# Gram's blocks written as products with ones, and running sums that begin with two tiles

## The chip, the cores and the metric

The kernel runs on one core of a Trainium2 chip. The metric is the device time of one execution in microseconds (us). Three runs of the kernel before gave 2723.8, 2724.28 and 2724.82 us; the median is 2724.28.

## What is computed

Eight images of 768 channels and 32 x 32 pixels go through two residual layers in float32. Cut to what matters:

```
h   = groupnorm(x)                        # 32 groups
k,v = h W_k, h W_v                        # 12 heads of 64; q is not needed
s   = var(v) var(k)^T / 8                 # one number per token and head: an outer product
x  += softmax(s) v  W_proj + b
f   = groupnorm(x)
c_o = sum_channels fn(p + o) fn(p)        # fn: f with unit norm, 28 offsets o in a 7 x 7 window
x  += [f, c] W_conv + b
```

The scores are an outer product of two vectors, so a tile of exponentials is one activation of a broadcast row with a per-partition scale. The softmax's denominators are sums of exponentials over keys. The correlations c are read from the diagonals of small Gram products of f with shifted windows of itself.

## The kernel before

**Staging.** The images are processed one after the other, with the stages of neighbours interleaved. In stage b the attention of image b, the second half of its keys and values, and the second layer (Gram products, then the convolution) of image b - 1 share the engines; "stage" always means this b, 0 to 8. TensorE (PE) runs the large products in a Strassen form with seven products in place of eight; sums of blocks for it are made by GpSimd (POOL) in `make_sums` (L579, instructions at L584 to L590) or by VectorE (DVE). ScalarE (ACT) makes the exponentials (L721). DVE takes results out of PSUM, does statistics and adds up denominators; its calls pass through a timing wrapper, so all of them carry line L152.

**Order.** The program is laid out by a planner in Python: `Clock` keeps a planned time for PE, ACT and DVE, units of work are emitted when their planned inputs are ready, and evacuations are emitted at planned due times. What the planner emits is a fixed order on each engine's queue; each queue runs in order, and semaphores make it wait for its operands. So a changed planned duration or a changed buffer release can reorder instructions on every queue.

**Attention.** A pair is two heads. `products(t)` (L740) multiplies the exponential tiles of key block t (two tiles of 128x1024) with the values, 8 matmuls in the trace, and eight blocks make a pair. `run` (L951) emits four blocks at a time, called a run of four here, and puts units of other stages between the runs. The pool of exponential tiles has six buffers (L175), three blocks' worth, so the exponentials of block t + 3 need the tiles of block t; `free_at` (L958) tells the planner when that will be. The denominators are had in two ways. For some pairs ACT makes the exponentials a second time, transposed, with a summed output (L731). For the summed pairs (L47: pairs 0, 3, 4, 5 of the first image, 3, 4, 5 of the others, 25 in all), DVE adds the eight tiles of each head into an accumulator `acc`, a copy for the first (L757) and seven additions (L759), and PE adds up its partitions at the end (`den`, L779 and L829). The accumulators take the buffers `bk` of the second exponentials (two, L174).

**Gram.** `turn(t)` (L1053) copies a block of 128 tokens of f, all six channel groups, into a tile in which the left and right halves of the image rows lie apart: two POOL copies of 128x384 (L1065), one for each half; the last image uses ACT. There is one such buffer (L176). `gram(t)` (L1067) multiplies the turned block with windows of f (L1080, 24 matmuls) and then emits the turn of block t + 1, which so waits for PE to be done with block t. Eight grams of an image lie between attention runs and units of keys and values. After grams 3 and 7, `diagonals` gathers the diagonals through DRAM and `scale` (L1119) turns the squared norms into reciprocal roots: a POOL `pow` on 128x4 (`rn`, L1125), then DVE makes the columns `dn`, and PE transposes them (`ct`, L1136).

**POOL's libraries.** The maximum over partitions in `spread` (`most`, L661) is a partition all-reduce of POOL. In the built kernel an instruction without a tile stands in front of each such all-reduce and in front of the first `tensor_tensor` after it: a change of POOL's instruction library. A POOL `tensor_copy` after the all-reduce has no such instruction in front. In stages 2 to 7 the first `tensor_tensor` after the all-reduce for the first half of the heads (`most_0`) is `rn` of the first four grams, behind the copies of turns 1 to 5:

```
POOL queue, before:  most_0 | turn_1 .. turn_5 (copies) | library change | rn_0 | turn_6
```

Of the kernel before, what the change touches and what calls it, by code (L numbers as in the profile page):

```python
# [8 lines left out]
ALU = mybir.AluOpType  # L9
# [7 lines left out]
J = C // P  # L17
# [11 lines left out]
HW = W // 2  # L29
# [42 lines left out]
def windows(ap, *dims):  # L72

    return bass.AP(tensor=ap.tensor, offset=ap.offset, ap=[list(d) for d in dims])
# [83 lines left out]
def two_layers(ctx, tc, x, wkv, wproj, bproj, wconv, wcorr, bconv, out):  # L158
    nc = tc.nc
# [29 lines left out]
    vector = Vector(nc.vector, clock)  # L189
# [23 lines left out]
    def act_copy(us, to, at):  # L213
        nc.scalar.copy(to, at)  # L214
        clock.act = max(clock.act, clock.now) + us
# [15 lines left out]
    class WeightSums:  # L231


        def __init__(self, which, *queues):
            self.which = which
            flat = image_tile(fpool, "f", f"ws{which}").rearrange("p j n -> p (j n)")
            self.at = [flat[:, n * JH * KW : (n + 1) * JH * KW] for n in range(5)]
            for n in range(4):
                r, c = divmod(n, 2)
                queue = queues[n % len(queues)]  # L240
                if which in (0, 1):
                    queue.dma_start(out=self.at[n].rearrange("p (k m) -> p k m", k=JH), in_=kv_block(which, r, c))
                else:
                    to = self.at[n].rearrange("p (k m) -> p k m", k=JH)
                    queue.dma_start(out=to, in_=t_block(which, r, c).rearrange("p k i m -> p k (i m)"))
# [145 lines left out]
    ones = const.tile([P, HD], F32, name="ones")  # L391
# [14 lines left out]
    rows = [dconst.tile([NROW, ROW], F32, name=f"rows{i}") for i in range(2)]  # L406
# [6 lines left out]
    def mask_rows():  # L413
        nc.gpsimd.memset(mask, 1.0)
        nc.gpsimd.memset(across, 1.0)
        at = 0
        for _, right, count in RUNS:
            run = across[:, at : at + count] if at else across[:, 0 : count - 1]
            right, count = (right, count) if at else (1, count - 1)
            for base, sign in ((right, 1), (W - 1 - right, -1)):  # L420
                nc.gpsimd.affine_select(
                    out=run, in_=run, compare_op=ALU.is_ge, fill=0.0, base=base,
                    pattern=[[sign, count]], channel_multiplier=sign,
                )
            at += count
        for q in range(P // HW):
            side = q // (P // W)
            nc.sync.dma_start(out=mask[q * HW : (q + 1) * HW, 1:], in_=across[side * HW : (side + 1) * HW, :])
# [262 lines left out]
    class Pair:  # L691
        def __init__(self, b, hp, kv, ot, before):
            half = hp // 3
            self.before, self.finished = before, False
            self.b, self.hp, self.half, self.vt, self.ot, self.kv = b, hp, half, kv.vt[hp], ot, kv
            self.summed = hp in SUMMED[b > 0]
            self.rows_at = {}
            self.over, self.rd_at, self.bk_free, self.out_at = False, None, False, None
            self.exs, self.bc, self.bk = {}, [], []
            self.passes = {"e": 0, "s": 0}  # L700
# [39 lines left out]
        def products(self, t):  # L740
            if t == 0:
                self.av = avp.tile([P, 2, HF], F32, tag="av", name=f"av{self.b}_{self.hp}")
            exs = self.exs.pop(t)
            for hf in range(2):
                for e in range(2):
                    nc.tensor.matmul(  # L746
                        self.av[e * HD : (e + 1) * HD, hf, :], lhsT=self.vt[:, t, e, :],
                        rhs=exs[e][:, hf * HF : (hf + 1) * HF], start=t == 0, stop=t == MT - 1,
                    )
            if t == MT - 1:  # L750
                later.after(STEP_US + 0.2, self.evacuate)
            if self.summed:
                if t == 0:
                    self.acc = [bkpool.tile([P, N], F32, tag="bk", name=f"acc{self.b}_{self.hp}_{e}") for e in range(2)]
                for acc, ex in zip(self.acc, exs):
                    if t == 0:
                        vector.tensor_copy(acc, ex)  # L757
                    else:
                        vector.tensor_tensor(acc, acc, ex, ALU.add)  # L759
                if t == MT - 1:  # L760
                    later.after_dve(0.5, self.sum_up if self.hp < HP - 1 else self.sum_up_last)
            if t == MT - 1:
                self.over = True
                self.try_finish()
# [108 lines left out]
    class Attention:  # L873
# [77 lines left out]
        def run(self):  # L951
            hp, t0 = divmod(self.done, MT)
            for t in range(t0, t0 + STEPS):
                while t not in self.pairs[hp].exs:
                    clock.pass_time(0.25)
                pair = self.pairs[hp]
                pair.products(t)
                self.free_at.append(max(clock.now + STEP_US, clock.dve - EXP if pair.summed else 0.0))  # L958
                self.done += 1
                clock.pass_time(STEP_US)  # L960

# [87 lines left out]
    class Corr:  # L1049
# [3 lines left out]
        def turn(self, t):  # L1053

            last = self.b == NB - 1
            pl, tag = (expool, "ex") if last else (turnpool, "turn")
            flat = pl.tile([P, N if last else J * P], F32, tag=tag, name=f"turn{self.b}_{t}")[:, : J * P]
            self.turned[t] = flat.rearrange("p (j s m) -> p j s m", j=J, s=2)
            to = flat.rearrange("p (j s y x) -> p j s y x", j=J, s=2, x=HW)
            rows = self.f[:, :, t * P : (t + 1) * P].rearrange("p j (y s x) -> p j y s x", y=4, s=2)  # L1060
            for side in range(2):
                if last:
                    act_copy(0.5, to[:, :, side], rows[:, :, :, side, :])
                else:
                    nc.gpsimd.tensor_copy(to[:, :, side], rows[:, :, :, side, :])  # L1065

        def gram(self, t):  # L1067

# [353 lines left out]
    for b in range(NB + 1):  # L1422
# [6 lines left out]
        if b:  # L1429
# [3 lines left out]
            f, acc = layer1[b - 1] if b > 1 else first_f * 2  # L1433
# [75 lines left out]
```

## Time and profile before

| | |
|---|---|
| median of 3 runs | 2724.28 us |
| profiled execution | 2723.3 us |
| its span on the core | 2721.6 us |
| PE busy | 2649.8 us (97%) |
| DVE busy | 1632.4 us (60%) |
| ACT busy | 1365.4 us (50%) |
| POOL busy | 355.3 us (13%) |
| granted PE clock, mean | 0.992 of full speed |

The span is from the first to the last instruction of the profiled execution; what lies around it is 1.7 us in that execution. The profile's groups name the operation by line, engine and tiles (buffer numbers left out), and tell how long the engine was idle before it and what ended that idle time. "Issue" is idle time that no semaphore of the profile explains. Matmuls are pipelined and their ends are modelled, so PE counts as busy over small gaps between matmuls.

### The profile page before, as it was taken

Reading aid. Unit: us, or ns where it says so; the run is one execution under the profiler, and the core shown is the slowest. Engines: PE = TensorE matmul, PEld = TensorE weight load, DVE = VectorE, ACT = ScalarE, POOL = GpSimd, SP = SyncE. Lnnn points to the kernel's source line nnn. Section 1 sums busy time; section 2 is a strip of 40 time slices with the busy share of each in tenths; the row PEclk is TensorE's granted clock in tenths of the full one; section 3 lists DMA queues with packets and bytes.
Section 4 is the critical chain, followed back from the end, with each engine's and each line's share of the span. In section 5 each row is a group of like instructions: output and inputs, shape, how many; then the busy total and the mean of one; then the engine's idle time right before and its main releaser. Section 6 shows DMA issues by size and latency. Waiting matters only on the chain.

```text
span 2721.6 us, 30651 instructions
## 1 busy us (share of the span) xinstructions
PE 2649.8 (97%) x9831; PEld 1230.9 (45%) x9831; DVE 1632.4 (60%) x4160; ACT 1365.4 (50%) x1841; POOL 355.3 (13%) x442
## 2 busy tenths in 40 slices
PE   7999999999999999999999999999999999999999
PEld 4443454345543454434544345443454434544344
DVE  5859734775347853478524875258742587525864
ACT  1497078700697006970079701796017960189600
POOL 4220120003200032000320012200122001220000
PEclk9999999999999999999999999999999999999999
DMA  7764456354553645626556365462654626545243
GB/s 275 297 233 134 142 191 179 105 201 154 158 180 112 205 152 157 194 90 210 158 153 191 92 208 167 141 205 79 223 167 139 189 82 230 172 116 158 86 127 101
DMA packets 323355, 446.04 MB, mean 164 GB/s; under 512 B 59458, under 2 KB 245170, under 8 KB 323194
## 3 DMA queue, kind: packets, MB, share of 16 engines
q1 hardware_dynamic: 321962, 441.32, 50.9%
q10 hardware_dynamic: 1232, 2.75, 0.3%
q8 instruction: 79, 1.29, 0.2%
q14 instruction: 82, 0.67, 0.1%
HBM read 377.49 MB, written 64.40 MB: 162 GB/s over the span
## 4 chain that ended last, share of the span: by engine, by line
PE 89%; DMA 5%; issue 3%; DVE 2%; ACT 1%; POOL 1%; SPq 0%; DVEq 0%; POOLq 0%; ACTq 0%
PE x L359 35%; PE av L746 22%; PE y L359 17%; PE z L359 9%; PE gr L1080 3%; DMA x<-x1d 1%; DMA di<-ir 1%; PE den L779 1%; DMA rd<-di 1%; PE x L988 1%; PE den L829 1%; PE y L988 1%; DMA vdr<-rsv 1%; PE z L988 1%; ACT ex L721 0%
## 5 line engine op out<-in xcount | busy, mean ns | idle before, releaser
L721 ACT ACTIVATE ex<-bc,nk 128x1024 f32<-128x1024 f32 x768 | 826.8, 1137 | 449.1 <-DMA bc<-vdr 227.0
L746 PE MATMUL av<-ex,v 128*64 128x512 f32 x3072 | 705.3, 604 | 4.8 <-ACT ex L721 4.6
L731 ACT ACTIVATE junk<-bk,vm 128x1024 bf16<-128x1024 f32 x368 | 420.4, 1142 | 42.1 <-DMA bk<-kdr 22.8
L746 PEld LDWEIGHTS av<-ex,v 128*64 128x64 f32 x3072 | 230.5, 138 | 442.7 <-issue 380.1
L152 DVE TENSOR_TENSOR acc<-acc,ex 128x1024 f32<-128x1024 f32 x350 | 402.0, 1215 | 0.0
L214 ACT COPY kp<-x 128x384 f32<-128x384 f32 x28 | 13.4, 478 | 559.2 <-PE x L359 559.2
L359 PE MATMUL y<-kv,s 128*128 128x384 f32 x744 | 260.7, 491 | 0.0
L359 PE MATMUL x<-kv,xn 128*128 128x384 f32 x756 | 257.1, 490 | 2.8 <-DVE xn L152 1.6
L359 PE MATMUL x<-kv,s 128*128 128x384 f32 x744 | 254.3, 489 | 0.0
L359 PEld LDWEIGHTS x<-kv,xn 128*128 128x128 f32 x756 | 144.1, 191 | 106.0 <-issue 7.1
L359 PEld LDWEIGHTS x<-kv,s 128*128 128x128 f32 x744 | 138.7, 190 | 101.9 <-issue 9.1
L359 PEld LDWEIGHTS y<-kv,s 128*128 128x128 f32 x744 | 137.8, 190 | 94.8 <-issue 7.3
L480 POOL TENSOR_TENSOR rstda<-vea,neghalf 128x1 f32<-128x1 f32 x8 | 4.8, 595 | 1009.9 <-DVE vea L152 1009.9
L359 PE MATMUL x<-v,wt 128*128 128x512 f32 x288 | 130.2, 596 | 0.0
L359 PE MATMUL z<-kv,xn 128*128 128x384 f32 x372 | 126.9, 488 | 0.0
L152 DVE TENSOR_TENSOR v<-y,v 128x128 f32<-128x128 f32 x180 | 40.9, 282 | 137.5 <-PE y L359 137.5
L359 PE MATMUL x<-f,wt 128*128 128x512 f32 x252 | 116.2, 601 | 1.9 <-DVE x L152 1.8
L584 POOL TENSOR_TENSOR s<-xn 128x384 f32<-128x384 f32 x64 | 68.0, 1070 | 290.2 <-PE x L359 202.2
L152 DVE BATCH_NORM_STATS2 vbn<-v 128x6 f32<-128x64 f32 x720 | 101.8, 211 | 0.0
L152 DVE COPY win<-gr 128x133 f32<-128x133 f32 x64 | 18.4, 288 | 128.2 <-PE gr L1080 118.6
L1065 POOL COPY turn<-f 128x384 f32<-128x384 f32 x112 | 54.5, 514 | 305.4 <-PE gr L1080 292.2
L152 DVE SCALAR_TENSOR_TENSOR x<-x,bconv_sb,x 128x512 f32<-128x512 f32 x63 | 45.8, 746 | 78.1 <-DMA x<-x1d 55.9
(191 smaller groups left out, 3040.3 us busy)
## 6 DMA issues: line engine op xcount, KB each, us to landing
kv<-kvs SPq DMA_DIRECT2D x124, 576.0 KB
kv<-in_wkv_dram SPq DMA_DIRECT2D x95, 576.0 KB
bc<-vdr SPq DMA_DIRECT2D x96, 512.0 KB
f<-in_x_dram SPq DMA_DIRECT2D x48, 512.0 KB
bk<-kdr SPq DMA_DIRECT2D x46, 512.0 KB
x1d<-f SPq DMA_DIRECT2D x42, 512.0 KB
x<-x1d SPq DMA_DIRECT2D x42, 512.0 KB
out_dram<-x SPq DMA_DIRECT2D x82, 256.0 KB
```

The costliest lines, as they stand in the source:

```text
L152: return getattr(self.engine, name)(*args, **kw)
L214: nc.scalar.copy(to, at)
L359: nc.tensor.matmul(t, lhsT=lhsT, rhs=rhs, start=p in FIRST and k == 0, stop=stop and k == len(pairs) - 1, skip_group_check=True,)
L584: nc.gpsimd.tensor_tensor(self.sums[g][:, 0], a[g][2], a[g][3], ALU.add)
L721: nc.scalar.activation(ex, self.bc[e], AF.Exp, scale=self.kv.nk[self.half][:, h, t : t + 1])
L731: nc.scalar.activation(junk, self.bk[e], AF.Exp, scale=self.kv.m2[self.half][:, h, t : t + 1], accum_out=self.sums[:, e, t : t + 1],)
L746: nc.tensor.matmul(self.av[e * HD : (e + 1) * HD, hf, :], lhsT=self.vt[:, t, e, :], rhs=exs[e][:, hf * HF : (hf + 1) * HF], start=t == 0, ...
L779: nc.tensor.matmul(den[at * 32 : (at + 1) * 32, :], lhsT=ones[:, 0:32], rhs=self.acc[e][:, hf * HF : (hf + 1) * HF], start=True, stop=True,)
L829: nc.tensor.matmul(den[e * HD : (e + 1) * HD, :], lhsT=ones, rhs=self.acc[e][:, at], start=True, stop=True)
L988: nc.tensor.matmul(t, lhsT=wcorr_sb[at, i, :], rhs=cs[at, tokens, :], start=False, stop=True, skip_group_check=True)
L1065: nc.gpsimd.tensor_copy(to[:, :, side], rows[:, :, :, side, :])
L1080: nc.tensor.matmul(ps[side * HD : (side + 1) * HD, :n].rearrange("p (y x) -> p y x", x=WIDE), lhsT=block[:, j, side, :], rhs=image[:, 4 * ...
```

## The change

In `turn`, the POOL copy becomes a POOL product of the same block with a tile of ones, read with a stride of zero over the six channel groups. In a summed pair, the copy of the first tile into the accumulator is gone: the addition at block 1 reads the tiles of blocks 0 and 1 and writes the accumulator. So the tiles of block 0 are now read by DVE at block 1, and the planner is told that they come free when those of block 1 do.

```
 class Pair:
-            self.before, self.finished = before, False
+            self.before, self.finished, self.first = before, False, []
 # products(t)
             if self.summed:
+                before = list(self.first)
                 if t == 0:
                     self.acc = [bkpool.tile(...) for e in range(2)]
                 for acc, ex in zip(self.acc, exs):
-                    if t == 0:
-                        vector.tensor_copy(acc, ex)
-                    else:
-                        vector.tensor_tensor(acc, acc, ex, ALU.add)
+                    if t:
+                        vector.tensor_tensor(acc, before.pop(0) if t == 1 else acc, ex, ALU.add)
+                self.first = exs
 # run()
                 self.free_at.append(max(clock.now + STEP_US, clock.dve - EXP if pair.summed else 0.0))
+                if pair.summed and t == 1:
+                    self.free_at[-2] = self.free_at[-1]
 # turn(t)
                 else:
-                    nc.gpsimd.tensor_copy(to[:, :, side], rows[:, :, :, side, :])
+                    half = rows[:, :, :, side, :]
+                    nc.gpsimd.tensor_tensor(to[:, :, side], half, windows(ones, ones.ap[0], (0, J), (HW, 4), (1, HW)), ALU.mult)
```

In the built kernel after the change, the library change of stages 2 to 7 stands directly behind `most_0` and in front of turn 1, and none is left in front of `rn_0`:

```
POOL queue, after:   most_0 | library change | turn_1 .. turn_5 (products) | rn_0 | turn_6
```

PE's order is the same in every stage up to the last runs of its attention. From pair 3 on (in stage 0 from pair 0 on) units of the convolution or of keys and values move by one to a few places: in stages 2 to 6 the eight blocks of pair 5, which stood in one piece of 64 matmuls, are now two runs of 32 with a unit between, and in stages 0 and 7 the same happens to pair 4.

## The prediction

> **What bounds the kernel now.** I read the page first. PE is busy 97% of a span of 2721.6 us and the chain that ended last is 89% PE, so time can come only from PE's gaps or from PE running slowly.
>
> ```profile
> PE 2649.8 (97%) x9831; PEld 1230.9 (45%) x9831; DVE 1632.4 (60%) x4160; ACT 1365.4 (50%) x1841; POOL 355.3 (13%) x442
> ```
>
> Second, the view of waits: for PE alone, and then over all engines for the last line.
>
> ```profile
> PE ct L1136 <- DVE dn L152: 33.4, 6, 6.2
> PE pma L465 <- DVE mva L152: 14.1, 1, 14.1
> PE av L746 <- ACT ex L721: 4.6, 4, 2.2
> PE den L779 <- DVE acc L152: 3.8, 2, 2.5
> PE gr L1080 <- POOL turn L1065: 2.9, 1, 2.9
> ...
> POOL rn L1125 <- issue: 45.5, 6, 8.2
> ```
>
> Columns: total us, times, longest. Nearly half of PE's 72 us of idle time is one transpose, `ct`, six times; 14.1 is the start. Behind `dn` stands POOL's `rn`, six times late for no semaphore ("issue"), 7.6 us each. Third, the timeline of stage 2, POOL and then PE (start, duration):
>
> ```profile
> 683.90 0.43 POOL L661 PARTITION_ALL_REDUCE most<-top  x1 [7.43 <-DVE top L152]
> 688.71 0.95 POOL L1065 COPY turn<-f 128x384 f32<-128x384 f32 x2 [4.37 <-PE gr L1080]
> ...
> 721.59 0.96 POOL L1065 COPY turn<-f 128x384 f32<-128x384 f32 x2 [8.49 <-PE gr L1080]
> 730.46 1.05 POOL L1125 TENSOR_TENSOR rn<-m,neghalf 128x4 f32<-128x4 f32 x1 [7.92 <-issue]
> ```
> ```profile
> 694.67 1.58 PE L1080 MATMUL gr<-f,turn 128*64 128x133 f32 x24
> ...
> 721.27 5.32 PE L746 MATMUL av<-ex,v 128*64 128x512 f32 x24
> 732.49 0.41 PE L1136 MATMUL ct<-ident,dn 128*80 128x128 f32 x1 [5.90 <-DVE dn L152]
> 732.83 3.19 PE L746 MATMUL av<-ex,v 128*64 128x512 f32 x8
> 735.86 1.53 PE L1080 MATMUL gr<-f,turn 128*64 128x133 f32 x24
> ```
>
> The turn's copies end at 722.55 and `rn` starts 7.92 later. That is where the built kernel has its library change. Also, the eight matmuls after `ct` take 3.03 us to the next row's start, where a quarter of a run of 32 (7.02) is 1.76. Fourth, the busy times by stretch (us; busy PE, PEld, DVE, ACT, POOL; granted clock; DMA) say why: the clock is 0.57 there, 0.50 to 0.57 in all six places.
>
> ```profile
> 721.20:726.20 5.00, 5.00 (x30) 1.64 (x24) 0.84 (x4) 3.02 (x4) 0.96 (x2) 1.00 0.44 162
> 732.40:735.90 3.50, 3.41 (x11) 1.09 (x13) 0.28 (x1) 0.00 (x0) 0.00 (x0) 0.57 0.09 26
> ```
>
> **What the Trainium skill says.** GPSIMD Engine Reference, 2.1 Instruction dispatch: the first call to a freshly loaded kernel pays about 6 us of load that shows as no instruction. The trace agrees in kind; here it is 7.2 to 8.2 us. The same page, 3.1 Elementwise: about 2.6 cycles for each element of a two-input operation, 1.03 for a simple one-input one. The trace: 1007 ns (two inputs, L590) and 514 ns (the copy), both 128x384. TensorE: Matmul & The Clock Gate, Part 1: after an idle window of about 3.4 us PE falls to half rate until it has been busy as long; the 0.57 above agrees. VectorE: DVE Perf Modes, the perf-mode tier table: an fp32 copy in SBUF runs at 2x, a tensor_tensor at 1x; 689 against 1220 ns (median) here.
>
> **Part 1, the library change moves.** Removed: one change of 7.2 to 8.2 us in front of `rn`, in six stages. In stage 2 the new `rn` starts when turn 5 is done: 721.59 + 2 x 1.01 = 723.6. It ends 1.05 later at 724.65. From the end of `rn` to `ct` takes 0.98 now (731.51 to 732.49), so `ct` could start at 725.65, and PE gets there at 732.49 - 5.90 = 726.59. Nothing is left of the wait, with 0.9 us to spare. In all six stages PE reaches `ct` 5.0 us after turn 5 starts. The gain is read from the first of the 24 matmuls to the gram after the eight: 14.59, 14.05, 15.32, 14.55, 14.02 and 14.28 us in the six stages, 86.8 in all; undisturbed it is a run of 7.02 and a transpose of 0.13 or so, 43 for six. Gain **43.6**: 33.4 of wait, the rest the slow clock after it. I take 43.
>
> Added: the change behind `most_0`. The all-reduce ends at 684.33; the change carries no wait of its own, so it starts there and ends at 691.5 to 692.5. Turn 1 waits behind it, 2.0 us for two products, until 693.5 to 694.5; gram 1 starts at 694.67. Hidden by the units of keys and values that PE has there, with 0.2 to 1.2 us to spare. Only turn 1 and gram 1 wait behind it on POOL, and all six stages have the same distance (10.8 us from all-reduce to gram 1). I put 0.1 us each, **+0.6**; if the change took 1 us more here, +5.
>
> **Part 2, products for copies.** 112 POOL instructions by 1007 - 514 = 493 ns is 55 us more on an engine at 13%. Covered where PE has other work before the next gram, which is 3 us or more after a turn nearly everywhere (694.67 and the next one 7.5 later, say). Not covered: the first gram of stage 1 (the wait of 2.9 on the turn), +1.1 for two slower halves, and its gram 2 (+0.1). The product with a zero-stride operand is not in the trace of before: bounds 0.8 us (2.6 cycles for 384 elements without dispatch) and 1.5 us (the slowest copy, 1500 ns); at 1.5 the six gram 1 would each wait 0.0 to 0.8 and `ct` 0.1. I take 1.01. **+1.2**.
>
> **Part 3, no copies into the accumulator.** 50 copies by 0.69 is 34.5 us less on DVE, which bounds no stage. The addition at block 1 costs what it did; only an operand differs. So directly nothing. Two indirect effects:
>
> *The tile of block 0 is held longer.* In a summed pair with run start T, steps on PE last 1.76. DVE first clears two evacuations and a reciprocal (to T + 1.6), adds head 0 to T + 2.8 and head 1 to T + 3.95. ACT's exponentials of block 3 (1.14 each) then end at T + 4.05 and T + 5.2; now the first starts at T + 2. PE needs them at T + 5.27 and about T + 5.5. It fits by 0.3 us. If that cover is gone, each 1 us costs 25 pairs by 1. The later blocks: block 6 is ready at T + 11.65 and needed at T + 13.4; `den` of pair 3 needs the last addition at T + 18.4 and PE comes at T + 20.6. I walked pairs 4 and 5 likewise in the order of the built kernel and found no wait.
>
> *The order of PE's queue.* The planner counts a copy at 1.2 us, so 2.4 us of planned DVE time go per pair, and runs and units move by a few places. PE's work is the same; what changes is whether a pair of 64 matmuls stands in one piece, where ACT (2.14 us per block by its rows) cannot follow PE (1.76):
>
> ```profile
> 1201.68 7.09 PE L746 MATMUL av<-ex,v 128*64 128x512 f32 x32
> ...
> 1212.46 14.94 PE L746 MATMUL av<-ex,v 128*64 128x512 f32 x64
> ```
>
> To the next row's start it is 14.87, against 2 x 7.02: 0.83 lost. Four of stages 2 to 6 lose 0.83, the fifth 15.77 - 14.04 = 1.73; all five are split now. **-5.0**. Pair 4 of stage 7 loses 15.76 - 14.04 = 1.7 with its wait for the accumulator; split, **-1.7**. In stage 0 pair 4 stood in one piece too (17.7 with 2.5 waiting for `acc`); in two runs with 3.9 us of units between, DVE's 16.1 of additions and some 2.5 of evacuations end 0.8 us after PE: **-3**. The new order may have waits that I haven't found; I take back 2.
>
> **The sum.** -43 + 0.6 + 1.2 - 9.7 + 2 = -49 on the span of 2721.6. The execution around it was 2723.3, the median 2724.28, 1.0 more. So 2724.3 - 49 = 2675.3; I say **2676**.
>
> **Rivals.** (a) *The change turns into a wait at gram 1.* For it: less than 1 us to spare, and DMA is half busy around 684 to 692. Against it: the change ran at a like DMA load (0.41 to 0.46) where it stood. With 1 to 2 us in six stages, 5 to 12: 2681 to 2688. (b) *Only the wait goes, and the reordered attention gives nothing* (new small waits at held tiles equal what the splits gain): -43 + 2 to -33 + 2, 2683 to 2693. (c) *Slower: held tiles.* DVE is in order, so if a reciprocal of 1.7 us or a DMA-bound one stands before the additions of block 1, block 3 comes late in each summed pair. It decides from (43 + 8) / 25 = 2 us per pair, that is if DVE starts those additions 2.3 us later than I walked. Against it: DVE idles 5.12 us in front of pair 4's copies in stage 2. At 3 us: 25 x 2.7 = 68, less 49, is 2743. (d) *The library change isn't what made `rn` late*, and it stays late behind slower turns: -9.7 + 2 + 1.2, and 1 us more at each of six `ct`, 2724. Against it: of 16 `rn` only the six with a change in front have this gap.
>
> **Chances.** Forecast 0.66; (a) 0.14; (b) 0.16; (c) 0.02; (d) 0.02. The range from 2666 (no waits at all and stages 0 and 7 gaining more) to 2692 holds the forecast and nearly all of (a) and (b), some 0.86. Within 0.2% (5.4 us), about what a measurement here can tell from no change, only (d) falls: faster 0.96, same 0.02, slower 0.02.
>
> **What would show it.** Right: `ct` gone from PE's waits, no "issue" in front of `rn`, granted clock near 1 after `ct`, some 7 us of idle in front of turn 1 behind `most_0`, gram 1 not later than 10.8 us after the all-reduce. Wrong: PE waits for `turn` six times (a), for `ex` or `acc` in runs of pairs 3 to 5 (b, c), or `rn` still late (d).

## The result and the profile after

The changed kernel took 2679.46 us (median of 4 runs, 2675.76 to 2680.35), beside 2724.04 for the kernel before (2719.56 to 2724.82). The ratio is 0.9837, with a 95% interval of 0.982 to 0.9854. The forecast was 2676, and the interval times 2724.04 runs from 2675 to 2684. A second set of runs gave 2679.13 and a ratio of 0.9844 (0.983 to 0.9859). The profiled execution took 2675.76 us around a span of 2674.0, so it is the shortest of the first four runs and flatters the change a little.

The page of the kernel after, busy time by engine:

```profile
PE 2634.8 (99%) x9831; PEld 1221.7 (46%) x9831; DVE 1604.2 (60%) x4110; ACT 1364.0 (51%) x1841; POOL 410.8 (15%) x442
```

POOL is busy 55.5 us longer with its 112 products, and DVE 28.2 us shorter without its 50 copies. PE is busy 15.0 us *shorter* with the same 9831 instructions: part of the gain is matmuls that run faster, not waits that are gone. The view of waits of the kernel after, for PE (us in total, times, longest):

```profile
PE pma L465 <- DVE mva L152: 13.8, 1, 13.8
PE av L746 <- ACT ex L721: 5.6, 4, 2.8
PE gr L1083 <- POOL turn L1068: 3.9, 2, 3.4
PE x L359 <- DVE x L152: 3.4, 7, 0.5
...
PE den L779 <- DVE acc L152: 1.2, 1, 1.2
```

`ct`, the first line of this view before, is gone. The start (`pma`) is what it was. The wait for `turn` has grown by 1.0 us and is met twice, not six times. PE's waits for `x` from DVE have grown, from three (1.8 us) before to seven (3.4 us). The timeline of stage 2, POOL and then PE (start, duration):

```profile
683.12 0.43 POOL L661 PARTITION_ALL_REDUCE most<-top  x1 [7.43 <-DVE top L152]
691.27 1.97 POOL L1068 TENSOR_TENSOR turn<-f,ones 128x384 f32<-128x384 f32 x2 [7.72 <-issue]
...
720.81 1.97 POOL L1068 TENSOR_TENSOR turn<-f,ones 128x384 f32<-128x384 f32 x2 [7.47 <-PE gr L1083]
722.74 1.06 POOL L1128 TENSOR_TENSOR rn<-m,neghalf 128x4 f32<-128x4 f32 x1
```
```profile
693.89 1.58 PE L1083 MATMUL gr<-f,turn 128*64 128x133 f32 x24
...
720.49 5.32 PE L746 MATMUL av<-ex,v 128*64 128x512 f32 x24
725.74 0.31 PE L1139 MATMUL ct<-ident,dn 128*80 128x128 f32 x1
725.97 1.94 PE L746 MATMUL av<-ex,v 128*64 128x512 f32 x8
727.74 1.53 PE L1083 MATMUL gr<-f,turn 128*64 128x133 f32 x24
```

The 7.72 us of idle time without a semaphore now stand in front of turn 1, and `rn` follows turn 5 at once. Turn 1 ends at 693.24 and gram 1 starts at 693.89, so 0.65 us were to spare; gram 1 is 10.77 us behind the start of the all-reduce, as before (694.67 - 683.90). The eight matmuls after `ct` take 1.77 us to the next row's start, and the busy times by stretch (PE, PEld, DVE, ACT, POOL; granted clock; DMA) show why:

```profile
725.40:728.90 3.50, 3.50 (x33) 1.90 (x33) 0.29 (x1) 3.50 (x7) 0.00 (x0) 1.00 0.80 226
```

The granted clock is 1.00 here, where it was 0.57. "Half clock" below means a stretch in which the trace's record of the granted clock reads 0.50.

### The profile page after: what moved, and what is told of

It is laid out like the page before. It is cut to its first block, busy times and chain, and to the rows that moved or that the text cites. A ratio compares the mean times of both kernels' runs of the same rounds, so it can differ in the third digit from the quotient of the medians.

```text
span 2674.0 us, 30536 instructions
## 1 busy us (share of the span) xinstructions
PE 2634.8 (99%) x9831; PEld 1221.7 (46%) x9831; DVE 1604.2 (60%) x4110; ACT 1364.0 (51%) x1841; POOL 410.8 (15%) x442
## 4 chain that ended last, share of the span: by engine, by line
PE 93%; DMA 4%; DVE 2%; issue 0%; ACT 0%; SPq 0%; POOL 0%; DVEq 0%; POOLq 0%; ACTq 0%
PE x L359 36%; PE av L746 24%; PE y L359 17%; PE z L359 9%; PE gr L1083 3%; DMA x<-x1d 1%; PE den L779 1%; PE x L990 1%; PE y L990 1%; PE z L990 1%; DMA vdr<-rsv 0%; DMA x1d<-f 0%; DVE x L152 0%; DVE v L152 0%; PE den L829 0%
## 5 line engine op out<-in xcount | busy, mean ns | idle before, releaser
L746 PE MATMUL av<-ex,v 128*64 128x512 f32 x3072 | 691.7, 597 | 5.6 <-ACT ex L721 5.6
L746 PEld LDWEIGHTS av<-ex,v 128*64 128x64 f32 x3072 | 223.4, 137 | 434.8 <-issue 372.4
L152 DVE TENSOR_TENSOR acc<-acc,ex 128x1024 f32<-128x1024 f32 x300 | 344.7, 1211 | 0.0
L1068 POOL TENSOR_TENSOR turn<-f,ones 128x384 f32<-128x384 f32 x112 | 111.6, 1016 | 265.9 <-PE gr L1083 206.5
L359 PEld LDWEIGHTS z<-kv,xn 128*128 128x128 f32 x372 | 69.9, 190 | 49.2 <-issue 2.3
```

The lines of the kernel that those rows point to most:

```text
L152: return getattr(self.engine, name)(*args, **kw)
L359: nc.tensor.matmul(t, lhsT=lhsT, rhs=rhs, start=p in FIRST and k == 0, stop=stop and k == len(pairs) - 1, skip_group_check=True,)
L746: nc.tensor.matmul(self.av[e * HD : (e + 1) * HD, hf, :], lhsT=self.vt[:, t, e, :], rhs=exs[e][:, hf * HF : (hf + 1) * HF], start=t == 0, ...
L1068: nc.gpsimd.tensor_tensor(to[:, :, side], half, windows(ones, ones.ap[0], (0, J), (HW, 4), (1, HW)), ALU.mult)
```

## The experiments

The kernels ran in four groups, each on one chip with the kernel before beside it, whose medians were 2723.49, 2721.39, 2721.87 and 2723.16 us. Kernels of different groups are compared by their distance from it. Each kernel starts from the one before or the one after, with the edit shown.

**The products alone.** Only the part of the change in `turn` is made, and the copies into the accumulators stay. PE's order is that of before.

> Only Gram's blocks as products with ones (parts 1 and 2); the copies into the accumulators stay, and PE's order is that of before. The prediction's theory (the moved library change takes the wait at ct away, the reordered attention gives the rest): 43 us less, 1.8 more for the slower turns, so 2683 us; ct gone from PE's waits, pair 5 of stages 2 to 6 still one piece that loses 0.8 to 1.7 us. Rival (the products as such give everything, the sums nothing): 2679, like the full change. Rival (the library change isn't the cause): 2724 or more.

Measured: 2683.12 us (2680.13 to 2686.23), ratio 0.9849 (0.9835 to 0.9862), 40.4 less than before. The prediction has -41.2 for parts 1 and 2.

**The sums alone.** All of the change is made except its part in `turn`: the running sums begin with two tiles, and the turns stay copies. PE's order is that of after.

> Only the running sums that begin with two tiles (part 3); the turns stay copies, so the library change stays in front of rn, and PE's order is that of the full change. The prediction's theory: the six waits at ct stay (33 us in all, half clock after them) and only the split pairs gain, -9.7 + 2, so about 2716 us. Rival (the attention's order gives nothing): 2724. Rival (held tiles cost time): over 2726.

Measured: 2725.15 us (2716.74 to 2726.53), ratio 1.0 (0.9991 to 1.0008): nothing, where 7.7 us less was expected. The wait at `ct` stays (view of waits, sums alone):

```profile
PE ct L1138 <- DVE dn L152: 32.3, 6, 6.0
```

To find where the gain went, I summed the times from one matmul's start to the next's, by product, over stages 2 to 6 (from one `most_0` to the next), and divided by five. Per stage, before and sums alone:

```
                 before   sums alone   difference
attention av      92.18      91.39       -0.79
Gram gr           11.16      11.71       +0.55
conv. y<-f         8.30       8.91       +0.61
conv. x<-t4f       8.02       8.32       +0.30
it                 0.33       0.43       +0.10
whole stage      335.61     336.41       +0.80
```

The split pairs do gain: 0.8 us in each stage here, and 0.7 in the kernels below that have no wait at `ct` (84.85 to 84.16 us of `av` with the tiny product). The Gram's 0.55 is the half clock after `ct`, which lasts 6.83 us in all six stages here and in three of six before. In the row `y<-f` two waits of PE for a tile `x` from DVE are hidden. The first stands in front of `x<-f`, 124 to 133 us behind `most_0`. It comes and goes between executions of one kernel, in either order: 2.6 us over stages 2 to 7 before, 2.1 here, 5.9 and 1.2 in two executions of the products alone. The second is new, and the reordering makes it. The timeline of stage 2, DVE and then PE, in the kernel before:

```profile
895.29 1.22 DVE L152 TENSOR_TENSOR v<-v,rd 128x1024 f32<-128x1024 f32 x1
899.61 1.76 DVE L152 RECIPROCAL acc<-den 128x256 f32<-128x256 f32 x1 [3.10 <-PE den L829]
901.28 0.63 DVE L152 TENSOR_TENSOR x<-z,x 128x512 f32<-128x512 f32 x1
901.83 0.68 DVE L152 TENSOR_TENSOR x<-x,x 128x512 f32<-128x512 f32 x1
```
```profile
903.00 2.74 PE L359 MATMUL x<-t4f,wt 128*128 128x512 f32 x6
```

The same place with the sums alone:

```profile
902.80 1.76 DVE L152 RECIPROCAL acc<-den 128x256 f32<-128x256 f32 x1 [4.54 <-PE den L829]
904.49 1.23 DVE L152 TENSOR_TENSOR v<-v,rd 128x1024 f32<-128x1024 f32 x1
905.63 0.68 DVE L152 TENSOR_TENSOR x<-z,x 128x512 f32<-128x512 f32 x1
906.24 0.68 DVE L152 TENSOR_TENSOR x<-x,x 128x512 f32<-128x512 f32 x1
```
```profile
906.97 2.84 PE L359 MATMUL x<-t4f,wt 128*128 128x512 f32 x6 [0.61 <-DVE x L152]
```

Before, DVE does the product `v<-v,rd` in front of the reciprocal, in time in which it would idle for `den` anyway; the result tile `x` is out at 902.51, half a microsecond before PE is there. In the new order the product stands behind the reciprocal, the idle time grows from 3.10 to 4.54, and `x` is out 4.12 us after the reciprocal's start where it was 2.90. PE, which comes to the tile at about the same distance, waits. This place loses 0.67 to 0.84 us in each of stages 2 to 7 in all five profiled executions with the new order, and nothing in the nine with the old one. The 0.30 of `x<-t4f` and the 0.10 of `it` come with the new order every time, too; they were not traced further. Together that is 1.1 us a stage.

**The place of the library change alone.** One tiny product, read by nobody, behind the all-reduce; all turns stay copies.

```
+    primed = const.tile([P, 4], F32, name="primed")
 # spread, behind the all-reduce
+            nc.gpsimd.tensor_tensor(primed, neghalf, neghalf, ALU.mult)
```

> The kernel before with one POOL product of 128x4 directly behind the all-reduce, whose result nobody reads; turns stay copies, nothing else changes. If the place of the library change alone is what matters: the change of 7 to 8 us starts at the end of the all-reduce, rn follows turn 5 at once, ct is gone from PE's waits, 43 us less: 2681 us. If the products of the turns do something else than to pull the library change ahead: 2724.

Measured: 2682.09 us (2679.58 to 2684.43), ratio 0.9844 (0.9831 to 0.9858), 41.4 less. The 112 products aren't needed: one instruction of the other library at that place does the same. The timeline of POOL in stage 2:

```profile
685.85 0.43 POOL L662 PARTITION_ALL_REDUCE most<-top  x1 [7.43 <-DVE top L152]
694.15 0.19 POOL L663 TENSOR_TENSOR primed<-neghalf 128x4 f32<-128x4 f32 x1 [7.87 <-issue]
694.30 0.95 POOL L1067 COPY turn<-f 128x384 f32<-128x384 f32 x2
...
723.54 0.96 POOL L1067 COPY turn<-f 128x384 f32<-128x384 f32 x2 [8.49 <-PE gr L1082]
724.46 1.06 POOL L1127 TENSOR_TENSOR rn<-m,neghalf 128x4 f32<-128x4 f32 x1
```

**The tiny product and the sums.** Both edits above together.

> The small POOL product behind the all-reduce and the running sums that begin with two tiles; turns stay copies. Everything the full change gains without the slower turns: the full change's time less 1 to 2 us (the wait of the first grams of stages 1), so 2676 to 2679 us against 2679.5. If the slower turns cost something that the waits don't show, up to 10 us less than the full change.

Measured: 2682.36 us (2679.63 to 2683.44), ratio 0.9842 (0.9829 to 0.9856). That is above the 2676 to 2679 us expected: again the sums add nothing (+0.3 us against the tiny product alone, on the same chip).

**The sums' share once more, on one chip.** The full change and the products alone were run again, with a third kernel: the full change in which the planner goes on charging for the copies that are gone, so that PE's order is that of before.

```
+                    if t == 0:
+                        clock.dve = max(clock.dve, clock.now) + 0.15 + 0.00104 * N
                     if t:
                         vector.tensor_tensor(acc, before.pop(0) if t == 1 else acc, ex, ALU.add)
 # run()
-                if pair.summed and t == 1:
-                    self.free_at[-2] = self.free_at[-1]
```

> The full change once more, beside the next two. Expected near 2679.5 us as before. If the sums' share is what the first runs say (nothing alone, nothing on top of the small product), it equals turn_again within 3 us; if the prediction's -7.7 holds, it is 8 us below it.

> Only the products in the turns (as turn_only), on the same chip as the full change, so that the sums' share is a difference on one chip: 2683 us, that is 0 to 4 us above the full change if what the split pairs gain is given back at other waits, 8 above it by the prediction.

> The full change, but the planner goes on charging 1.2 us of DVE for each copy that is no longer there, and frees the tiles of block 0 as before, so PE's order is that of before: the sums without the reordering. If the reordering is all that the sums do to PE: equal to turn_again, within 2 us. If 34.5 us less of DVE work gains by itself (evacuations that come earlier): 3 to 6 us below turn_again. If held tiles cost time in an order that was planned without them: above turn_again.

Measured: full change 2679.13 (2677.93 to 2682.51), products alone 2680.31 (2677.45 to 2684.64), sums in the old order 2680.78 us (2679.0 to 2682.6); ratios 0.9844, 0.9848 and 0.9851, each known to 0.0016 or so. The three can't be told apart. So taking 28 us of DVE's work away, the reordering, and the longer held tiles in an order planned without them each come to nothing that these runs can tell from zero.

**The wait taken away on PE, POOL untouched.** The kernel before, with `ct` emitted later: behind the rest of its run, the next gram and a unit of keys and values.

```
-                later.after_dve(0.7 if b else 4.0, lambda: to_dram(dn))
+                later.after_dve(9.5 if b else 4.0, lambda: to_dram(dn))
```

> The kernel before with the transpose ct emitted later: behind the rest of its run of 32, the next gram and a unit of keys and values. POOL's queue is untouched, so rn stays late by the library change, but PE doesn't wait for it. If the time is lost through ct alone: 33 us of wait and 9 of half clock gone, 43 us less, 2681 us. If something else that is late behind rn or the library change (turn 6, the diagonals, the convolution's inputs) also holds PE up: above 2690, with a new wait on PE that names it.

Measured: 2684.03 us (2681.1 to 2687.47), ratio 0.9861 (0.9845 to 0.9876), 37.4 less. In stages 2 to 6 it gains 8.1 us each (327.47 against 335.61), more than the full change (328.26); but from the last `most_0` to the start of PE's last matmul it is slower than any other, 357.5 us against 345.2 for the full change. The view of waits for PE names the place:

```profile
PE cc L1257 <- DMA cs<-cs: 3.0, 1, 3.0
PE cc L1257 <- issue: 2.0, 1, 2.0
```

In the last image the convolution stands right behind the Gram products, and the later `ct` brings the correlations (`cs`) late. Of the 11.2 us against the same stage with the old `ct` (346.3, in the last experiment) these two waits are 5.0; most of the rest is half clock, which the trace shows from 2658.65 to 2672.31.

**A wait put back, in two sizes.** The kernel with the tiny product, and in front of `rn`, in the six stages, eight or fourteen POOL products of 128x96 whose results nobody reads.

```
+            for _ in range(8 if hf == 0 and 1 <= b <= 6 else 0):      # or 14
+                nc.gpsimd.tensor_tensor(waste, self.f[:, 0, 0:96], self.f[:, 0, 0:96], ALU.mult)
```

> The kernel with the small product behind the all-reduce, and eight products of 128x96 in front of rn in each of the six stages, whose results nobody reads; estimated 0.35 to 0.5 us each, 2.8 to 4.0 us, of which 1.0 is slack: a wait at ct of 1.8 to 3.0 us, put back in the place of the old one. If a wait under 3.4 us costs only itself: 11 to 18 us over the kernel with the small product alone, and the eight matmuls after ct take 1.8 us at a granted clock near 1. If every wait at ct brings the half clock: 9 us more, 20 to 27, and 3 us for the eight matmuls.

> The same with fourteen such products: 4.9 to 7.0 us, a wait at ct of 3.9 to 6.0 us. The time comes back as it was in the kernel before: 23 to 36 us of wait, and by the half clock 1.2 to 1.6 us more in each stage, 31 to 45 in all over the kernel with the small product alone; the eight matmuls after ct take near 3 us.

Measured: with eight, 2688.21 us (2685.63 to 2694.0), ratio 0.9871 (0.9852 to 0.989), 33.7 below before; with fourteen, 2714.32 us (2711.09 to 2716.7), ratio 0.9966 (0.9954 to 0.9978), 7.6 below. Against the 41.4 of the tiny product alone they cost 7.7 and 33.8. The slack was 2.0 us, not 1.0: I had taken it from the slower products, and with copies turn 5 ends 1.0 earlier. So the eight (3.33 us) make waits of 1.2, below what I expected. PE around `ct` with eight, its stretch, and the same with fourteen:

```profile
726.75 0.28 PE L1141 MATMUL ct<-ident,dn 128*80 128x128 f32 x1 [1.24 <-DVE dn L152]
726.96 1.94 PE L749 MATMUL av<-ex,v 128*64 128x512 f32 x8
728.73 1.53 PE L1083 MATMUL gr<-f,turn 128*64 128x133 f32 x24
```
```profile
726.90:728.70 1.80, 1.80 (x9) 0.63 (x10) 0.29 (x1) 1.74 (x3) 0.00 (x0) 1.00 0.71 250
```
```profile
730.05 0.28 PE L1141 MATMUL ct<-ident,dn 128*80 128x128 f32 x1 [3.80 <-DVE dn L152]
730.26 2.87 PE L749 MATMUL av<-ex,v 128*64 128x512 f32 x8
732.90 2.34 PE L1083 MATMUL gr<-f,turn 128*64 128x133 f32 x24
```
```profile
730.00:732.80 2.80, 2.75 (x9) 0.95 (x11) 0.29 (x1) 0.00 (x0) 0.00 (x0) 0.70 0.09 21
732.90:735.20 2.30, 2.30 (x27) 2.12 (x23) 0.00 (x0) 2.04 (x4) 0.00 (x0) 0.64 0.73 223
```

After 1.24 us of idle time the clock is 1.00 and the matmuls take what they always do. After 3.80 us it is 0.70 and 0.64 in the mean of two stretches. PE doesn't restart slow: within them the record reads 1.00 up to 731.1 and then 0.50 for 3.41 us, up to 734.5. The eight `av` and the 24 `gr` matmuls behind `ct` take 1.77 + 1.46 = 3.23 us undisturbed. With fourteen they take 1.67 to 1.69 more in five stages and 2.66 in one, where the half clock lasts 6.82 us, 11.1 us in all; with eight, none. Both prices fit: six waits of 7.5 us in all against 7.7 measured, and 22.8 us of waits + 11.1 = 33.9 against 33.8. (They fit better than the runs can tell: each distance is known to 3 to 5 us.) The old wait is thus shown part by part: POOL's delay in front of `rn`, less the slack, is PE's wait, and a wait of 3.80 us brought the half clock in all six stages. But "a wait under 3.4 us costs only itself" doesn't hold: in the kernel with eight, a wait of 2.61 us for `x` in stage 3 (1137.98 to 1140.59) is followed by 3.41 us of half clock.

**A later `ct` where it pays.** The late `ct` only for images 1 to 6, in the kernel before and in the kernel after.

```
-                later.after_dve(0.7 if b else 4.0, lambda: to_dram(dn))
+                later.after_dve(9.5 if 1 <= b <= 6 else 0.7 if b else 4.0, lambda: to_dram(dn))
```

> The transpose ct later in the Grams of images 1 to 6 alone (stages 2 to 7), and in its old place for image 7, whose late ct had made PE wait 5 us for the correlations at the end. POOL's queue and the sums are those of the kernel before. If the 11 us that the late ct lost after stage 6 were that wait and what follows on it: 11 less than with all ct late, about 2673, below the full change, without touching POOL. If they were something else: about 2684.

> The full change with the transpose ct later in images 1 to 6. The full change has no wait at ct left, so moving it can save only PE's switch into and out of it (0.1 to 0.3 us in each of six stages) and what the shifted evacuations do to the waits of the convolution: 2677 to 2680 us if that is nothing, 6 us less if the short waits for evacuations of the convolution go, as they did with the late ct in the kernel before.

Measured: 2672.31 us (2671.03 to 2675.34), ratio 0.9812 (0.9798 to 0.9826), in the kernel before; 2675.62 us (2675.02 to 2678.09), ratio 0.9824 (0.9811 to 0.9838), in the kernel after. The first of these, one changed line in the kernel before, has the lowest median of the study, as expected (about 2673). Its stage 7 takes 346.3 us where all `ct` late took 357.5, so the loss was there. In both kernels the first wait of `y<-f`, in front of `x<-f`, is gone in all stages, as with all `ct` late; with the tiny product it takes 1.4 us a stage in stages 2 to 6. That is most of what this kernel gains over the tiny product there (327.38 against 329.13 us a stage). POOL and PE of stage 2 in it:

```profile
718.93 0.96 POOL L1065 COPY turn<-f 128x384 f32<-128x384 f32 x2 [8.49 <-PE gr L1080]
727.48 1.05 POOL L1125 TENSOR_TENSOR rn<-m,neghalf 128x4 f32<-128x4 f32 x1 [7.59 <-PE gr L1080]
728.51 0.94 POOL L1065 COPY turn<-f 128x384 f32<-128x384 f32 x2
```
```profile
725.48 1.53 PE L1080 MATMUL gr<-f,turn 128*64 128x133 f32 x24
726.94 2.20 PE L359 MATMUL z<-kv,xn 128*128 128x384 f32 x6
728.98 4.03 PE L359 MATMUL x<-kv,xn 128*128 128x384 f32 x12
732.85 0.27 PE L1136 MATMUL ct<-ident,dn 128*80 128x128 f32 x1
```

`rn` is as late as ever, 7.59 us behind turn 5. The profile names a gram as what released it, but `rn` doesn't read a gram: the name is only the semaphore event that came last before it. `ct` is needed 4.3 us after `rn` has ended, so nobody notices. A stage takes 327.38 us here and 327.80 in the kernel after with the same edit: the two kernels differ by av -0.68, y<-f +0.69, x<-t4f +0.30 and it +0.10, the bill of the sums without other waits. The remaining difference of these two executions lies in stage 1 (387.3 against 391.8 us from `most_0` to `most_0`), where grams wait for the slower turn (3.8 against 3.0 us) and the trace has three stretches of half clock, against none. Over the fourteen traces stage 1 takes 387.3 us with none of them, 389.2 with one, 389.5 to 391.0 with two and 391.8 to 393.8 with three. So part of the lead of the lowest median may be such stretches; the intervals of the two ratios overlap.

## Why the prediction held, and which of its terms did not

**Part 1, the library change moves: right.** Moved without anything else, it gave 41.4 us less against -43 + 0.6. In the traces the attention's matmuls, which hold the wait and the half clock behind it, go from 92.18 to 84.85 us per stage in stages 2 to 6 with the tiny product, and from 93.50 to 86.58 in stage 7: 5 x 7.33 + 6.92 = 43.6. The prediction read 43.6, too (its six readings less 43 make 43.8). The named signs are all there: no `ct` among the waits, nothing in front of `rn`, clock 1.00, 7.72 us in front of turn 1, gram 1 at the same distance. The spare time at `ct` was put at 0.9 us; with products it is 0.96 (`rn` ends at 723.80, 0.98 to `ct`, `ct` at 725.74). The spare time at gram 1 was put at 0.2 to 1.2 and is 0.65.

**Part 2, products for copies: small, as forecast, but a term was left out.** A product with the zero-stride operand took 1016 ns where 1.01 us was taken from the plain one. The waits of `gr` for `turn` grew by about the 1.2 us forecast: 3.8 to 4.8 us in the six profiled executions with products, 2.7 to 3.4 in the eight with copies. What the step left out is the clock behind the longer wait in stage 1: a stretch of half clock follows it in all six with products and in two of the eight with copies, and the Gram products of stage 1 take 12.75 to 13.34 us in those six against 11.52 to 12.72. Stage 1 took 390.4 to 393.8 us in the six (mean 392.1) and 387.3 to 390.7 in the eight (389.6), so the part cost some 2.5 us there. The products alone came out 1.0 us above the tiny product on the same chip, which is within their scatter.

**Part 3, the sums: this term was mis-sized.** The gains of the split pairs came: 0.7 us in each of stages 2 to 6, 3.4 in all where "-5.0" was booked, and 2.7 in stage 7 (`av` 86.58 to 85.00 us, `den` 4.98 to 3.86) where "-1.7" was. What failed is the take-back of 2 for "waits that I haven't found": I had walked PE's new order but not DVE's, in which `v<-v,rd` has moved behind a reciprocal, and the convolution and `it` give back 1.1 us in each of six stages, 6.5 in all. That makes +0.4. The -3 of stage 0 can't be found in the runs, whose stage 0 scatters by 3 us with either order. Together -7.7 was forecast, and three comparisons on one chip each gave +1.7 (the ratio's interval is -2.5 to +2.2 us), +0.3 and -1.2. The step "It fits by 0.3 us" for the held tiles held: PE waits 4.1 to 6.8 us for `ex` in all these executions, 4.6 before, and the sums cost nothing measurable even in the order that was planned without the longer hold.

**The rivals.** (a), a wait at gram 1, did not come. (b) is half of what happened: the reordered attention does give nothing, but the gain at `ct` came whole, so parts 1 and 2 alone, 2724.3 - 41.2 = 2683, would have been the better forecast by its terms. The measured 2679.46 and 2679.13 lie between 2676 and that, as near to the one as to the other. So the total held because part 1, which carries it, was right and the range was wide; that it came within 4 us although part 3's 7.7 wasn't there is luck. (c) and (d) fell: held tiles cost nothing measurable, and moving the library change alone brings the gain.

**What stays open.** The medians of the full change lie 1 to 4 us below the products alone, where the other two comparisons of the sums show no gain. The runs of one kernel scatter by 4 to 7 us, so this may be chance. The traces show two things that differ between executions of one kernel: the wait in front of `x<-f` (5.9 against 1.2 us) and the half clock of stages 0 and 1. Why the later `ct` takes that wait away was not traced.

## What to carry to other kernels

When an engine is late for no semaphore, look in its built queue for a change of state and ask which instruction triggers it: the same change can be had earlier with one tiny instruction, or the consumer can be emitted later, which here did at least as well (0.9812, 0.9798 to 0.9826, against 0.9844, 0.9831 to 0.9858, for the tiny instruction). Price a stall of PE as the wait plus the slow clock that may follow: here waits of 3.2 us and more always brought it, waits of 1.9 to 3.1 us sometimes, waits of 1.24 us never. When a planner reorders work around a gain, walk the other engines' new queues too before booking it: what a split of PE's run gained, a DVE product that had changed places gave back.

## What the runs showed of the hardware

- The library change took 6.6 to 8.5 us in every place it was put (in front of `rn`, of a turn, of a tiny product that itself takes 0.19), from the end of the POOL instruction ahead of it to the start of the one behind. It began when the all-reduce ended or, before, when turn 5 ended. Copies on POOL ran behind the all-reduce without it.
- The Trainium skill, TensorE: Matmul & The Clock Gate, Part 1, gives a window of about 3.4 us for both ways, and a free-running one. The traces agree on the window: the stretches of half clock last 3.41 us or a multiple of it, and within a trace they start at multiples of 3.41 us from each other, wherever PE stopped or restarted. A whole one loses 1.7 us, which five of six stages with fourteen products show as 1.67 to 1.69.
- They differ on what counts as idle: PE needn't stand still for a window. Cut into such windows, thirteen traces (all with a half clock, from 25 us on) have 46 windows at full clock in which PE was busy for less than 1.43 us, and half clock followed every one; it followed none of those with over 1.56 us, and nine of the twelve between. So in the kernel before two waits for `ex` in stage 1, of 2.24 and 1.90 us, brought it, and the wait of 2.91 us for `turn`, which fell across two windows, did not.
- A POOL product of 128x96 took 0.42 us from one start to the next (5.88 for fourteen), one of 128x384 0.97 (1.97 for two).
